# One-transfer gate fetches, variance scaling on GpSimd and a kept turned context in a four-layer transformer kernel

## The chip, the cores and the metric

The kernel runs on one core of a Trainium2 chip. The metric is the device time of one execution in microseconds (us); lower is better. The core has TensorE (PE; PEld is its weight load), VectorE (DVE), ScalarE (ACT), GpSimd (POOL) and SyncE (SP), which in this kernel issues every transfer, and 16 DMA engines that carry the transfers out.

## The reference: what is computed

All data is float32. `x` is 128 batches x 64 tokens x 128 features, `ctx` (the context) has the same shape, `cond` is one vector of 128 features for each batch. Four blocks follow each other, each with weights of its own:

```
L0:  x += P(attn(ada(x), ada(ctx)))                                   ada = layer norm, scaled and shifted by silu(cond) @ W
L1:  x += g*P(self_attn(ada(x)));  x += P(attn(ln(x), ln(ctx)));  x += g*gelu_mlp(ada(x))
L2:  x += g*P(self_attn(ada(x)));  x += g*P(top16_attn(ada(x), ctx));  x += g*swiglu_mlp(ada(x))
L3:  x += g*P(self_attn(ada(x)));  x += P(attn(ln(x), ctx));  x += g*gelu_mlp(ada(x))
```

Every attention has 16 heads of 8 features over 64 keys. The gates `g` depend on `cond`, so on the batch and the feature and not on the token. There are seven of them. L0 and L1 normalize the context, L2 and L3 take it raw.

## The kernel before

**Tiling.** A chunk is 8 batches, 512 tokens, so there are 16 chunks. Token-major tiles are [128, 4, 128]: partition = token of two neighbouring batches (64 tokens each), the middle index t = which pair of batches, then the feature. Feature-major ("turned") tiles are [128, 512]; `flip` (lines 612-621) makes one with four TensorE transposes. Most tiles come from a pool of 30 buffers of 256 KB named `some`; PSUM gives three slots named `mm`, two `ps` and one `po`.

**The order of the work** is not written out by hand. Each step is an `op(engine, cost, outs, ins, give, latency)`, given to a planner (`Plan`, lines 135-320) with a cost in ns and, for transfers, a latency. Eight lanes each work on one chunk and take the next when theirs runs out. `Plan.run` places, again and again, the step that can start first by those costs. It tries 48 seeds that vary the costs by 1% and keeps the shortest plan. Each engine then gets its instructions in the planned order, and keeps to it on the chip whatever the real durations are. Where the plan leaves TensorE idle for over 1000 ns, `warm` (line 1138) puts dummy matmuls into about half of the gap. Changing any cost, or taking any step out, so gives another order everywhere.

**A layer norm** is `moments` (line 633: two batch-norm statistics on DVE), then in `normal` one DVE instruction over 128x4 elements that makes variance + eps (line 645), a power of -1/2 on POOL (line 648, `minus_half` is a constant tile), four DVE instructions that normalize (line 653), and `flip`. `modulate` scales on DVE (line 662, out of PSUM) and shifts on POOL (line 663). There are 12 norms a chunk, two of them of the context.

**The context** is loaded from DRAM by `context` four times a chunk, once a layer (line 610). L0 and L1 take moments and normalize; L2 and L3 only flip it (tile `pc`) and copy it out of PSUM on ACT (line 1065).

**Attention** projects keys, queries and values, sends the queries through four transfers that spread them over a block tile (line 696, `qbd`), makes scores (line 741) and exponentials (line 752), or for the top-16 attention a chain of DVE maximum searches (lines 809-824), and weighs the values (line 871). Result and softmax sums leave PSUM on ACT (line 881), go to a DRAM tile `spill` (line 882) and come back by head (sums at line 899, values at line 903). DVE takes the reciprocal of the sums (line 906, tile `rec`), which goes to DRAM (line 908, `spillrec`) and comes back broadcast over the 8 features of a head (line 912: the DRAM side is walked as [16, 8 times the same, 512], the other side as 128 partitions). POOL multiplies (line 916). `watch` (lines 929-931) keeps on POOL, for a test at the end, a running sum of the reciprocals and a count of those above 2^-100. If the test fails, a slower safe version of the network runs as well; in the profiled run it did not.

**Gates.** `prepare` computes each of the seven gates once and stores it to DRAM as [128 batches, 2, 128]: part 0 is the gate, part 1 the gate times the projection's bias (line 550, one store a gate). `by_token` (lines 940-950) fetches one part for a chunk into a `some` tile, broadcast over the tokens. It issues two transfers on SP (line 947), one for the even and one for the odd batches, each walked as [64 times the same, 4, 128] on the DRAM side and 64 partitions on the other. `add` (line 962) uses part 1 on POOL, `residual` (lines 970-971) part 0 on DVE with a POOL addition behind it. That makes 14 fetches a chunk, 224 in all, as 448 transfers. The fetch of part 1 waits for the statistics of the norm ahead of it, that of part 0 for the reciprocal of the attention's sums or for the second half of the MLP.

Every transfer of the kernel goes through one queue that SP issues in the planned order, and SP waits at each transfer until what that transfer needs is there.

Of the kernel before, what the change touches and what calls it, by code (L numbers as in the profile page):

```python
# [21 lines left out]
NCHUNK = B // CB  # L22
NT = T // P
NPAIR = CB // 2
N_ATTN = 7
TOPK = 16
MLP = 512
LANES = 8
# [2 lines left out]
NSOME = 30  # L31
NQBD, NPROB, NVAL = 3, 8, 4
SCALE = 1.0 / math.sqrt(HD)
REC_HI, REC_LO = 2.0**64, 2.0**-100
GONE = -(2.0**126)


# [287 lines left out]
def kernel(ctx: ExitStack, tc: tile.TileContext, ins: dict, out: bass.AP, nchunk: int = NCHUNK):  # L325
# [13 lines left out]
        )  # L339


    ident = const.tile([P, P], F32, name="ident")
    make_identity(nc, ident)
    ones = const.tile([P, P], F32, name="ones")
    nc.gpsimd.memset(ones, 1.0)
    minus_half = const.tile([P, NT], F32, name="minus_half")
    nc.gpsimd.memset(minus_half, -0.5)


    cond_in = const.tile([P, D], F32, name="cond_in")  # L350
# [3 lines left out]
    bm1h = const.tile([P, NJ], F32, name="bm1h")  # L354
    scT = const.tile([P, B], F32, name="scT")
    dram = ctx.enter_context(tc.tile_pool(name="dram", bufs=1, space=bass.MemoryType.DRAM))
    gates_dram = [dram.tile([B, 2, D], F32, name=f"gates{n}") for n in range(len(GATES))]
    mods, W, plain, col, at = {}, {}, {}, {}, 0
    for name, n in BIASES:
        col[name] = at  # L360
# [21 lines left out]
    def prepare(plan, ready, all_of_it, vblocks, queries, pool, spills):  # L382
# [23 lines left out]
        def scratch(width):  # L406
            t = plan.tile(lambda: pool[t.slot][:, :width], "some")
            return t

        def mm(name):  # L410
            return plan.tile(lambda: mm_tile(name), "mm")
# [44 lines left out]
        for layer in range(4):  # L456
# [72 lines left out]
            for n, (key, i, w, b, bv) in enumerate(GATES):  # L529
                if key != of:  # L530
                    continue
                bname, kinds = next((bname, kinds.split()) for k, _, bname, kinds in CONDS if k == key)
                cw, g, p, done = weights[key, i - i % 4], scratch(2 * D), mm("pg"), plan.kept(True)

                def products(cw=cw, i=i, p=p, bname=bname, w=w, b=b, bv=bv):
                    nc.tensor.matmul(
                        p()[:, :D], lhsT=scT, rhs=cw()[:, i % 4 * P : (i % 4 + 1) * P], start=True, stop=False
                    )
                    spread_bias(p()[:, :D], bname, i, False)
                    added(p()[:, D : 2 * D], w, b, bv)  # L540

                def keep(g=g, p=p, half=kinds[i] == "half"):
                    nc.vector.tensor_copy(g()[:, :D], p()[:, :D])
                    nc.vector.tensor_tensor(g()[:, D:], g()[:, :D], p()[:, D : 2 * D], ALU.mult)
                    if half:
                        nc.vector.tensor_scalar_mul(g()[:, :D], g()[:, :D], 0.5)

                op(PE, 900, [p], [cw, sc, bi, biases, *([ready_w[w]] if w else [])], products, bulk=late)
                op(DVE, 600, [g], [p], keep, bulk=late)
                op(SP, 400, [done], [g], lambda n=n, g=g: nc.sync.dma_start(  # L550
                    out=gates_dram[n].rearrange("b k d -> b (k d)"), in_=g()
                ), 2500, bulk=late)
                parts.append(done)

            op(SP, 1, [ready[layer]], parts, lambda: None)
        return plan.ops
# [13 lines left out]
    def lane(n, plan, work, safe, acc, ready, vblocks, queries, pool, spills):  # L570
# [6 lines left out]
        def wop(engine, cost, outs, takes, *rest, **how):  # L577

            op(engine, cost, outs, [*takes, ready[layer[0]]], *rest, **how)

        def sb(shape, tag, bufs=1):
            name = f"{tag}{n}"
            return plan.tile(lambda: work.tile(shape, F32, tag=name, name=name, bufs=bufs), name, bufs)
# [31 lines left out]
        def flip(x, name):  # L615

            p = mm(name)

            def turn():
                for t in range(NT):  # L620
                    nc.tensor.transpose(p()[:, t * P : (t + 1) * P], x()[:, t, :], ident)  # L621

            op(PE, 460, [p], [x], turn)
            return p

        def moments(x):


            parts = sb([P, NT, 3], "parts")

            def stats():
                for t in range(0, NT, 2):
                    nc.vector.bn_stats(  # L633
                        parts()[:, t : t + 2, :].rearrange("p t k -> p (t k)"),
                        x()[:, t : t + 2, :].rearrange("p t d -> p d t"),
                    )

            op(DVE, 740, [parts], [x], stats)
            return parts

        def normal(x, mv, eps):

            rstd = sb([P, NT], "rstd", 2)

            op(DVE, 238, [rstd], [mv], lambda: nc.vector.tensor_scalar(  # L645
                rstd().unsqueeze(2), mv()[:, :, 2:3], 1.0 / D, eps, ALU.mult, ALU.add
            ))
            op(POOL, 1070, [rstd], [rstd], lambda: nc.gpsimd.tensor_tensor(rstd(), rstd(), minus_half, ALU.pow))  # L648
            xn = some([P, NT, D])

            def norm():
                for t in range(NT):
                    nc.vector.tensor_scalar(  # L653
                        xn()[:, t, :], x()[:, t, :], mv()[:, t, 1:2], rstd()[:, t : t + 1], ALU.subtract, ALU.mult
                    )

            op(DVE, 1480, [xn], [x, mv, rstd], norm)

            return flip(xn, "pn")
# [15 lines left out]
        def attention(hq, hkv, wq, bq, wk, wv, topk=False):  # L675
# [250 lines left out]
            if not safe:  # L926

                def watch():
                    nc.gpsimd.tensor_scalar(fits, recs(), REC_LO, None, ALU.is_ge)
                    nc.gpsimd.tensor_tensor(acc[0], acc[0], recs(), ALU.add)  # L930
                    nc.gpsimd.tensor_tensor(acc[1], acc[1], fits, ALU.add)

                op(POOL, 1080, sums[:2], [recs], watch)
                if topk:
                    op(POOL, 320, [sums[2]], [counts], lambda: nc.gpsimd.tensor_tensor(
                        acc[2], acc[2], counts(), ALU.add
                    ))
            return oT

        def by_token(n, part, c, behind):  # L940

            g = some([P, NT, D])

            def fetch():
                for e in range(2):
                    rows = gates_dram[n][c * CB + e : (c + 1) * CB : 2, part, :]
                    nc.sync.dma_start(
                        out=g()[e * S : (e + 1) * S], in_=rows.unsqueeze(0).to_broadcast([S, NT, D])
                    )

            wop(SP, 1300, [g], behind, fetch, 2500)
            return g

        def add(x, gate, c, parts):
# [89 lines left out]
        def chunk(c):  # L1044
# [10 lines left out]
            def scaled(key, scale, shift):  # L1055
                return mods[key, scale], mods[key, shift], c

            def context(behind, eps=None, *scaled):

                ct, ck = load(c_flat, c, behind=behind), some([P, T])  # L1060
                pn = flip(ct, "pc") if eps is None else normal(ct, moments(ct), eps)
                if scaled:
                    modulate(ck, pn, *scaled)
                else:
                    op(ACT, 585, [ck], [pn], lambda: nc.scalar.copy(ck(), pn()))
                return ck
# [63 lines left out]
    def network(lanes, safe, acc=None):  # L1130
        def warm(tile, ns):
# [4 lines left out]
            while columns > 0:  # L1136
# [2 lines left out]
                columns -= n  # L1139

        slots = {"mm": 3, "ps": 2, "po": 1, "qbd": 1 if safe else NQBD, "prob": 2 if safe else NPROB,
                 "values": 1 if safe else NVAL, "some": 10 if safe else NSOME, "spill": 1 if safe else LANES}

        def planned(seed, tc=None, work=None, *tiles):
            plan = Plan(tc, slots, warm, seed)
# [6 lines left out]
        with tc.tile_pool(name=f"work{int(safe)}", bufs=1) as work:  # L1152


            vblocks = []
            for k in range(slots["values"]):
                v = work.tile([P, NPAIR * NH * VW + 32 - VW], F32, tag=f"vbuf{k}", name=f"vbuf{k}", bufs=1)
                vblocks.append(v)

            queries = []  # L1160
            for k in range(slots["qbd"]):
                q = work.tile([P, 4, T], F32, tag=f"qbd{k}", name=f"qbd{k}", bufs=1)
                queries.append(q)
            pool = [work.tile([P, T], F32, tag=f"some{k}", name=f"some{k}", bufs=1) for k in range(slots["some"])]
            spills = [
                (
                    dram.tile([NG, P, 2, P], F32, name=f"spill{int(safe)}_{k}"),
                    dram.tile([NH, T], F32, name=f"spillrec{int(safe)}_{k}"),
                )
                for k in range(slots["spill"])  # L1170
            ]
            assert planned(seed, tc, work, vblocks, queries, pool, spills) < math.inf

    acc = [const.tile([P, m], F32, name=k) for k, m in (("recsum", 4 * NH), ("fitting", 4 * NH), ("taken", 8))]
    fits = const.tile([P, 4 * NH], F32, name="fits")
    for a in acc:
        nc.gpsimd.memset(a, 0.0)
    network(LANES, False, acc)
# [2 lines left out]

    ok = const.tile([P, 8 * NH + 8], F32, name="ok")
    nc.vector.tensor_scalar(ok[:, 0 : 4 * NH], acc[0], REC_HI, None, ALU.is_le)
    nc.vector.tensor_scalar(ok[:, 4 * NH : 8 * NH], acc[1], float(N_ATTN * nchunk), None, ALU.is_equal)
    nc.vector.tensor_scalar(ok[:, 8 * NH :], acc[2], float(8 * TOPK * nchunk), None, ALU.is_equal)
    ok1 = const.tile([P, 1], F32, name="ok1")
    nc.vector.tensor_reduce(ok1, ok, AX.X, ALU.min)
# [33 lines left out]
```

## Time and profile before

| what | value |
|---|---|
| median of 3 runs (lowest to highest) | 1953.83 us (1948.8 to 1966.26) |
| the profiled execution's own time | 1960.57 us |
| its span | 1958.8 us |
| granted TensorE clock, mean | 0.956 |
| ACT busy, share of the span | 1265.2 us, 65% |
| POOL busy | 1139.4 us, 58% |
| ctx loads | 64 of 256 KB |
| gate transfers | 448 of 128 KB, median 3.5 us from issue to landing |

How to read it: a line of a group gives the busy time of all its instructions, the mean of one, and the idle time of the engine just before them with what ended it. A matmul counts twice there when it runs in two passes. A line of a wait gives who waited for whom, the total in us, how often and the longest. "SPq" is the issuing of a transfer by SP; the time to landing is counted from there until its data has arrived. A table by stage gives for each stretch of the span the busy time of each engine, the granted clock, the mean busy share of the 16 DMA engines and the GB/s they moved.

### The profile page before, as it was taken

To read this page: it belongs to the slowest core of one execution; us is meant where nothing else is said; L and a number is where in the kernel's file an instruction comes from. 1 tells how busy PE (TensorE), PEld (TensorE's weight loads), DVE (VectorE), ACT (ScalarE), POOL (GpSimd) and SP (SyncE) were. 2 spreads that over 40 slices of the span, in tenths; PEclk is the share of its full clock that TensorE was granted. 3 is DMA by queue.
4 is the path that set the end of the run, shared out by engine and by line. 5 is a ranking of instruction groups with operands and counts; after the bars stand their busy time and mean duration, and the time that the engine had idled before them with its cause. 6 is when DMAs were issued, how large, how long until landed. Compare 5 with 4: busy or idle time off the path is not lost. (4 is left out here: it accounts for less than half of the span.)

```text
span 1958.8 us, 75790 instructions
## 1 busy us (share of the span) xinstructions
PE 1732.5 (88%) x30631; PEld 1198.4 (61%) x30631; DVE 1446.4 (74%) x6299; ACT 1265.2 (65%) x1842; POOL 1139.4 (58%) x1226
## 2 busy tenths in 40 slices
PE   6798899889898898889989898889988899988987
PEld 4566666666566665666666666556656666656554
DVE  7635354899999899998634578867869989997411
ACT  1567677676577465766668577666775777665542
POOL 6535375656646755667646566657557556656432
PEclk7999899999999899999999998999999999999999
DMA  7345555443236332555455554445453435334332
GB/s 207 101 141 152 154 150 154 132 116 110 83 89 182 97 99 73 158 147 146 139 156 142 156 149 130 126 135 140 118 166 94 114 105 143 116 91 121 105 92 61
DMA packets 385339, 249.40 MB, mean 127 GB/s; under 512 B 56076, under 2 KB 341076, under 8 KB 384980
## 3 DMA queue, kind: packets, MB, share of 16 engines
q1 hardware_dynamic: 384980, 244.46, 43.6%
q8 instruction: 244, 4.00, 0.9%
q14 instruction: 115, 0.94, 0.2%
HBM read 147.49 MB, written 67.50 MB: 110 GB/s over the span
## 5 line engine op out<-in xcount | busy, mean ns | idle before, releaser
L752 ACT ACTIVATE prob<-ps 128x1024 f32<-128x1024 f32 x384 | 377.5, 1023 | 110.6 <-PE ps L741 109.3
L653 DVE TENSOR_SCALAR some<-x,parts,rstd 128x128 f32<-128x128 f32 x640 | 260.2, 469 | 56.9 <-POOL rstd L648 53.3
L871 PEld LDWEIGHTS po<-prob,vbuf 128*32 128x32 f32 x14336 | 219.3, 112 | 97.1 <-issue 51.4
L871 PE MATMUL po<-prob,vbuf 128*32 128x64 f32 x14336 | 259.4, 225 | 6.3 <-ACT prob L752 3.5
L648 POOL TENSOR_TENSOR rstd<-rstd,minus_half 128x4 f32<-128x4 f32 x192 | 200.2, 1047 | 91.4 <-DVE rstd L645 78.2
L916 POOL TENSOR_TENSOR some<-some,some 128x512 f32<-128x512 f32 x112 | 144.3, 1290 | 177.7 <-DMA some<-spillrec 107.2
L741 PE MATMUL ps<-qbd,some 32*64 32x256 f32 x6144 | 229.6, 394 | 10.5 <-DMA qbd<-some 4.4
L839 POOL TENSOR_TENSOR some<-some,some 128x512 f32<-128x512 f32 x128 | 166.8, 1306 | 114.4 <-ACT some L831 113.0
L971 POOL TENSOR_TENSOR x<-x,some 128x512 f32<-128x512 f32 x112 | 146.0, 1304 | 108.6 <-DVE some L970 96.8
L811 DVE MATCH_REPLACE8 some<-m,some 128x64 f32<-128x64 f32 x1024 | 206.4, 209 | 0.3 <-issue 0.3
L962 POOL TENSOR_TENSOR x<-x,some 128x512 f32<-128x512 f32 x112 | 147.1, 1315 | 84.3 <-DMA some<-gates 30.3
L714 ACT COPY vbuf<-pv 64x512 f32<-64x512 f32 x224 | 153.8, 687 | 51.7 <-PE pv L707 49.4
L881 ACT COPY some<-po 128x512 f32<-128x512 f32 x224 | 131.8, 589 | 82.6 <-PE po L871 59.5
L813 DVE MAX8 m<-some 128x8 f32<-128x64 f32 x1024 | 177.0, 214 | 0.0
L809 DVE MAX8 m<-some 128x8 f32<-128x64 f32 x1024 | 172.1, 209 | 4.3 <-ACT some L789 4.3
L970 DVE TENSOR_TENSOR some<-py,some 128x512 f32<-128x512 f32 x112 | 76.5, 683 | 119.4 <-PE py L983 34.2
L741 PEld LDWEIGHTS ps<-qbd,some 32*64 32x64 f32 x6144 | 119.1, 133 | 74.2 <-issue 28.4
L906 DVE RECIPROCAL rec<-sums 128x64 f32<-128x64 f32 x112 | 61.0, 545 | 132.6 <-DMA sums<-spill 132.5
L663 POOL TENSOR_TENSOR some<-some,mod_L 128x512 f32<-128x512 f32 x112 | 118.2, 1057 | 55.2 <-DVE some L662 46.6
L621 PE MATMUL pn<-ident,some 128*128 128x128 f32 x768 | 128.2, 285 | 20.6 <-DVE some L662 5.6
L621 PEld LDWEIGHTS pn<-ident,some 128*128 128x128 f32 x768 | 91.3, 142 | 82.4 <-issue 24.4
L633 DVE BATCH_NORM_STATS2 parts<-x 128x6 f32<-128x256 f32 x320 | 120.2, 417 | 16.1 <-POOL x L971 14.3
(209 smaller groups left out, 3585.2 us busy)
## 6 DMA issues: line engine op xcount, KB each, us to landing
spill<-some SPq DMA_DIRECT2D x224, 256.0 KB, 3.6
some<-gates SPq DMA_DIRECT2D x448, 128.0 KB, 3.5
qbd<-some SPq DMA_DIRECT2D x448, 64.0 KB, 2.1
some<-spill SPq DMA_DIRECT2D x112, 256.0 KB, 3.6
some<-spillrec SPq DMA_DIRECT2D x112, 256.0 KB, 4.0
some<-in_ctx_dram SPq DMA_DIRECT2D x64, 256.0 KB, 4.5
x<-in_x_dram SPq DMA_DIRECT2D x16, 256.0 KB, 2.9
out_dram<-x SPq DMA_DIRECT2D x16, 256.0 KB, 2.4
```

Source lines behind the costliest of these rows:

```text
L621: nc.tensor.transpose(p()[:, t * P : (t + 1) * P], x()[:, t, :], ident)
L648: op(POOL, 1070, [rstd], [rstd], lambda: nc.gpsimd.tensor_tensor(rstd(), rstd(), minus_half, ALU.pow))
L653: nc.vector.tensor_scalar(xn()[:, t, :], x()[:, t, :], mv()[:, t, 1:2], rstd()[:, t : t + 1], ALU.subtract, ALU.mult)
L714: nc.scalar.copy(v4(vbuf())[rows, :, :, 0 : 2 * HD].rearrange("p m h (d b) -> p m h d b", b=2)[:, :, :, :, b], pv()[rows].rearrange("p (m ...
L741: nc.tensor.matmul(pscs[g // 2]()[b * S : (b + 1) * S, g % 2, u].rearrange("p (h q) -> p h q", h=4), lhsT=kT()[rows, cols], rhs=qbd()[rows ...
L752: op(ACT, 1020, [pr], [psc], lambda pr=pr, psc=psc: nc.scalar.activation(pr().rearrange("p g u h q -> p (g u h q)"), psc().rearrange("p g ...
L809: nc.vector.max(m1()[:, j, :], ex()[:, j, :])
L811: nc.vector.match_replace(w()[:, j, :], m1()[:, j, :], ex()[:, j, :], GONE)
L813: nc.vector.max(m2()[:, j, :], w()[:, j, :])
L839: op(POOL, 1310, [ex], [ex, w], lambda ex=ex, w=w: nc.gpsimd.tensor_tensor(ex(), ex(), w(), ALU.mult))
L871: nc.tensor.matmul(po()[32 * j : 32 * j + 32, g, u], lhsT=vbuf()[:, at : at + 32], rhs=prs[gp]()[:, gi, u, j], start=True, stop=True,)
L962: op(POOL, 1310, [x], [x, g], lambda: nc.gpsimd.tensor_tensor(x(), x(), g(), ALU.add), bulk=True)
```

## The change

Gates: the DRAM tile becomes [16 chunks, 2 parities, 2 parts, 4, 128], with the gate of the even and of the odd batches of a chunk lying apart, so each half of a token tile reads one run of 512 floats (2048 B). It is written by four stores a gate (28 instead of 7), and a fetch is one transfer: the DRAM side is walked as [2, 64 times the same, 512], the other side as 128 partitions. The planner's numbers for it go from 1300 + 2500 ns to 690 + 2800 ns.

Variance + eps moves from DVE to POOL, into one step with the power (1250 ns instead of 238 and 1070). `minus_half` is filled earlier.

Context: L0's moments of the context are kept for L1. L2 stores its turned context to DRAM (a tile `turned` for each lane), and L3 loads that instead of loading, flipping and copying again.

`watch` keeps a sum of the reciprocals and a sum of the softmax sums (two additions instead of a comparison and two additions); the test at the end becomes that both stay under a bound.

```diff
-    gates_dram = [dram.tile([B, 2, D], F32, name=f"gates{n}") for n in range(len(GATES))]
+    gates_dram = [dram.tile([NCHUNK, 2, 2, NT, D], F32, name=f"gates{n}") for n in range(len(GATES))]
...
-                op(SP, 400, [done], [g], lambda n=n, g=g: nc.sync.dma_start(
-                    out=gates_dram[n].rearrange("b k d -> b (k d)"), in_=g()
-                ), 2500, bulk=late)
-                parts.append(done)
+                for e in range(2):
+                    for k in range(2):
+                        part = plan.kept(True)
+                        op(SP, 500, [part], [g], lambda n=n, g=g, e=e, k=k: nc.sync.dma_start(
+                            out=gates_dram[n][:, e, k], in_=g()[e::2, k * D : (k + 1) * D]
+                        ), 2500, bulk=late)
+                        parts.append(part)
...
-            op(DVE, 238, [rstd], [mv], lambda: nc.vector.tensor_scalar(
-                rstd().unsqueeze(2), mv()[:, :, 2:3], 1.0 / D, eps, ALU.mult, ALU.add
-            ))
-            op(POOL, 1070, [rstd], [rstd], lambda: nc.gpsimd.tensor_tensor(rstd(), rstd(), minus_half, ALU.pow))
+            def root():
+                nc.gpsimd.tensor_scalar(rstd().unsqueeze(2), mv()[:, :, 2:3], 1.0 / D, eps, ALU.mult, ALU.add)
+                nc.gpsimd.tensor_tensor(rstd(), rstd(), minus_half, ALU.pow)
+
+            op(POOL, 1250, [rstd], [mv], root)
...
                 def watch():
-                    nc.gpsimd.tensor_scalar(fits, recs(), REC_LO, None, ALU.is_ge)
                     nc.gpsimd.tensor_tensor(acc[0], acc[0], recs(), ALU.add)
-                    nc.gpsimd.tensor_tensor(acc[1], acc[1], fits, ALU.add)
-
-                op(POOL, 1080, sums[:2], [recs], watch)
+                    nc.gpsimd.tensor_tensor(acc[1], acc[1], cs(), ALU.add)
+
+                op(POOL, 690, sums[:2], [recs, cs], watch)
...
             def fetch():
-                for e in range(2):
-                    rows = gates_dram[n][c * CB + e : (c + 1) * CB : 2, part, :]
-                    nc.sync.dma_start(
-                        out=g()[e * S : (e + 1) * S], in_=rows.unsqueeze(0).to_broadcast([S, NT, D])
-                    )
-
-            wop(SP, 1300, [g], behind, fetch, 2500)
+                rows = gates_dram[n][c, :, part].rearrange("e t d -> e (t d)")
+                nc.sync.dma_start(
+                    out=g().rearrange("p t d -> p (t d)"), in_=rows.unsqueeze(1).to_broadcast([2, S, NT * D])
+                )
+
+            wop(SP, 690, [g], behind, fetch, 2800)
...
+            seen, turned = [], plan.tile(lambda: spills[turned.slot][2], "turned")
+
             def context(behind, eps=None, *scaled):
 
+                if eps is None and turned.writer is not None:
+                    ck = some([P, T])
+                    op(SP, 500, [ck], [turned, *behind], lambda: nc.sync.dma_start(out=ck(), in_=turned()), 2600)
+                    return ck
                 ct, ck = load(c_flat, c, behind=behind), some([P, T])
-                pn = flip(ct, "pc") if eps is None else normal(ct, moments(ct), eps)
+                if eps is None:
+                    pn = flip(ct, "pc")
+                    op(ACT, 585, [ck], [pn], lambda: nc.scalar.copy(ck(), pn()))
+                    op(SP, 500, [turned], [ck], lambda: nc.sync.dma_start(out=turned(), in_=ck()), 2500)
+                    return ck
+                if not seen:
+                    seen.append(moments(ct, "seen"))
+                pn = normal(ct, seen[0], eps)
```

## The prediction

> **What bounds the kernel now.** I read the page's busy shares first, then the stages, then the waits, then the DMA lines.
>
> ```profile
> PE 1732.5 (88%) x30631; PEld 1198.4 (61%) x30631; DVE 1446.4 (74%) x6299; ACT 1265.2 (65%) x1842; POOL 1139.4 (58%) x1226
> ```
>
> TensorE is the busiest. 103.7 us of its time are the dummy matmuls of L1138. By stage (us; busy PE, PEld, DVE, ACT, POOL; clock, DMA share, GB/s):
>
> ```profile
> 100.00:400.00 300.00, 267.32 (x5432) 186.30 (x5431) 156.57 (x460) 211.84 (x292) 163.64 (x188) 0.96 0.52 148
> 400.00:900.00 500.00, 444.20 (x7954) 306.05 (x7955) 470.99 (x2474) 328.05 (x506) 308.66 (x316) 0.96 0.41 117
> 900.00:1200.00 300.00, 282.57 (x5289) 199.25 (x5288) 183.62 (x539) 215.34 (x299) 181.14 (x199) 0.97 0.51 146
> 1200.00:1500.00 300.00, 261.33 (x4886) 185.21 (x4878) 240.19 (x1098) 203.09 (x298) 183.69 (x201) 0.94 0.47 132
> 1500.00:1800.00 300.00, 269.72 (x4717) 188.32 (x4716) 274.74 (x1433) 205.97 (x313) 180.81 (x185) 0.97 0.41 116
> 1800.00:1959.00 159.00, 135.85 (x1520) 85.10 (x1518) 46.92 (x108) 64.61 (x89) 56.87 (x61) 0.95 0.29 84
> ```
>
> The reader is to see two co-limits, PE (about 90%) everywhere and DVE beside it in the top-16 stages (94% and 92%), and a DMA share near one half. That share is a mean over 16 engines: one engine can be full while it stays low.
>
> ```profile
> DVE rec L906 <- DMA sums<-spill: 132.5, 44, 12.3
> ...
> POOL some L916 <- DMA some<-spillrec: 107.2, 44, 7.1
> ...
> PEld py L983 <- POOL some L916: 92.4, 54, 6.0
> ```
>
> The attention's round trip through DRAM is already what DVE and POOL wait for most, and PE waits behind POOL: transfers have little slack.
>
> ```profile
> DMA packets 385339, 249.40 MB, mean 127 GB/s; under 512 B 56076, under 2 KB 341076, under 8 KB 384980
> ...
> q1 hardware_dynamic: 384980, 244.46, 43.6%
> ...
> some<-gates SPq DMA_DIRECT2D x448, 128.0 KB, 3.5
> ...
> some<-spillrec SPq DMA_DIRECT2D x112, 256.0 KB, 4.0
> ```
>
> And of the groups (line, shapes, times; busy us, mean ns; idle before):
>
> ```profile
> L645 DVE TENSOR_SCALAR rstd<-parts 128x4 f32<-128x4 f32 x192 | 63.1, 331 | 5.5
> ...
> L929 POOL TENSOR_SCALAR fits<-rec 128x64 f32<-128x64 f32 x112 | 45.6, 407 | 106.8 <-DVE rec L906 72.8 <-DVE m L809 21.3 <-DVE some L653 4.4
> ...
> L935 POOL TENSOR_TENSOR taken<-taken,counts 128x8 f32<-128x8 f32 x16 | 3.3, 204 | 9.3 <-DVE some L824 9.3
> ```
>
> From the packet counts one learns how many DMA engines a transfer uses. Of 56,076 packets under 512 B, 224 x 128 = 28,672 are the 256-byte pieces of the sums and of rec. That leaves 27,404 tiny closing packets. The program issues 1,713 transfers (1,671 of the groups named in the DMA view plus 42 loads of weights, cond and biases). At 16 each they would close with 27,408. Exactly four are missing. One transfer alone has a number of rows that 16 doesn't divide, the bias table with 72; the largest divisor of 72 up to 16 is 12. So a transfer is cut over a number of engines that divides its outermost count, and every other transfer of before has 16, 32, 64 or 128 there.
>
> **The change part by part.** Durations are of the profiled execution: span 1958.8, own time 1960.57, which is 0.3% above the median of 1953.83.
>
> *Gate fetch.* 448 transfers x 614 ns of issue (median of L947) leave SP and 224 come. Their issue costs about 546 ns (L912, the same size and also a broadcast), so SP issues 275 - 122 = 153 us less. SP waits for others anyway (267.9 us at L882 for ACT alone), so I book nothing on the path. The new source is walked as [2, 64, 512] and the target as 128 rows. If the outermost count decides as it did for the 72 rows, 2 is all that divides both sides, and one fetch of 262,144 B goes over two engines instead of 16. No transfer of before has 2 there, so the cost is bounded from both sides:
> - On 16 engines: the nearest row is spillrec, [16, 8, 512] onto 128 partitions, landing in 4.0 us. Against 3.5 that is +0.5 us a fetch, hidden: the two halves were issued one after the other, and one issue is now gone.
> - On two engines: 64 packets of 2,048 B on each. The trace's packet records give 84 ns (median) for such a packet, so 5.4 us. By the queue's mean, 0.436 x 16 x 1958.8 / 244.46 MB = 55.9 us per MB on one engine, 131,072 B take 7.3 us.
>
> I take two engines at 5.4 us: the packet count of this very trace shows the cut, and 2,048 B is the very packet size. Landing is then 3.5 + about 5 = 8.4 us. I assume that it is always the same two engines, which no row shows; with pairs that change no engine would fill, and the middle would be nearer to rival D.
>
> [...]
>
> Load of the two engines over the run: 224 x 5.376 = 1,204 us for gates (7.3: 1,635). The rest of the queue: 0.436 x 16 x 1958.8 = 13,665 us, minus the old gates (114,688 packets of 512 B at 28.9 ns = 3,313), minus 16 ctx loads (237), plus 32 turned transfers (344), over 16: 654 us. Sum 1,858 us, 95% of the span. By stage, with fetches counted by their users (L962 + L970: 35, 60, 36, 37, 39, then 17 at the end) and the rest from the DMA share minus 0.925 us a fetch for the old gates: 188 + 124 = 312 of 300; 323 + 150 = 472 of 500; 194 + 120 = 313 of 300; 199 + 107 = 306 of 300; 210 + 87 = 297 of 300. From 100 to 1800 us that is 1,700 us of work for 1,700 us. The other 14 engines fall to about 33%.
>
> No engine here keeps pace at 100%. All transfers share one queue, so qbd, spill, sums, rec and spillrec that are issued after a fetch stand behind it on these two engines, and SP, which waits in order, issues the next late. On POOL, an L962 that waits for its fetch holds the powers (L648), L916 and L663; on DVE, an L970 holds L653 and L906; PE waits for both. As the sustainable share I take what today's bound reaches: PE without dummies, (1,525 - 57) / 1,700 = 86% from 100 to 1800. The middle becomes 1,700 / 0.86 = 1,977 us (+277). In the last stage, 17 fetches land 4.9 us later each, between 0 and 83 us; of the 224 a user was seen waiting about 34 times, so about four count, +20. Ends: 95% share and nothing at the end, 1,789 in the middle (+89); 7.3 us a fetch, 1,700 + 207 x 1.92 = 2,098, at 86% 2,440 (+740); at 80% with 5.4 us, 2,125 (+425).
>
> *Gate stores*: 21 more x 0.33 us of issue (L550) = 7 us on SP in the first 110 us, between 0 and 7; SP's waiting there for DVE covers it; taken as 0.
>
> *Variance on POOL*: DVE loses 63.1 us. POOL gains 192 instructions between 204 ns (L935, 128x8, the nearest in size) and 407 (L929): 39 to 78 us. *Watch* takes 45.6 us (L929) away. POOL's net is -7 to +32 us on 1,139, no new bound. The power now stands behind POOL's queue already at the variance, which is 331 ns sooner done on DVE; in rank this is nothing beside 5 us.
>
> *Context kept*: 32 statistics x 0.417 = 13.4 us off DVE, 64 transposes = 10.0 us off PE, 16 ACT copies = 9.4 us off ACT. In the changed order ACT loads six tables more (67 against 61 in the work), 6 x 1.283 = 7.7 us back. 16 turned stores and 16 loads replace 16 ctx loads: counted above. Dummy columns fall from 49,222 to 46,944.
>
> What these small parts are worth where PE and DVE bound: 10.0 us on PE, and on DVE in the two top-16 stages 13.9 + 8.9 us (L645 there) and about 4 of the 13.4: up to 37 us, at least 0. With two DMA engines as the bound they are slack, and I book 0.
>
> Sum: 1,960.6 + 277 + 20 = 2,258 on the profiled execution; on the median's footing 2,250, and I say **2,240 us**, since part of the savings may count in the first and last stage.
>
> **The rivals.**
> - B, the other side: the fetch spreads over 16 engines as all wide transfers of before did. Then SP, DMA (3,313 us of packets become 2,408), DVE and PE all have less to do, and up to 37 us come off: 1,960 - 35 = 1,925. For it: spillrec is a broadcast and lands in 4.0 us. Against it: its outer count is 16. It decides if engines in use are more than about four: at four, a fetch takes 2.7 us on each and their load is 654 + 602 = 1,256 us, 64%, which fits.
> - C, the same but the savings lie beside PE's dummies and the planner's new order costs what it saves: within 1%, about 1,950. For it: PE stays near 90% and gives up 10 us.
> - D, two engines, but prefetch hides most: fetches are asked for well ahead of their use. Middle at 95% share: 1,960 + 89 = 2,050. Against it: the two engines delay every other transfer too.
> - E, the two engines move a byte as slowly as the queue's mean: up to 2,700.
>
> **How the numbers follow.** A with 2,240 has 0.70 (its own range 2,080 to 2,560), D 0.08, E 0.06, B 0.10, C 0.06. A measurement of this kernel tells about 1% from no change. Faster by over 1% is B, 0.10; within 1% is C, 0.06; slower by over 1% is A, D and E, 0.84. For 8 in 10 the range takes A nearly whole, D and the part of C above 1,950, and leaves out B and the top of E: 1,950 to 2,560.
>
> **What would show it.** Right: some<-gates x224 landing at 8 us or more; sums, spill and spillrec landing later than 2.4, 3.6 and 4.0; the waits of L906 and L916 for transfers grown several times; mean DMA share about 35 to 40% all the same; PE near 77%; closing packets 14 short of 16 for each of the 224 fetches. Small parts: L645 gone, a POOL instruction of about 0.2 us in its place. Wrong: gates landing near 4 us, or PE still near 90% with a longer span, which would put the blame on the new order.

## The result and the profile after

| what | before | after |
|---|---|---|
| median | 1955.5 us (1948.8 to 1966.26, 4 runs) | 2468.66 us (2465.04 to 2475.0, 4 runs) |
| ratio | 1 | 1.2621, 95% interval 1.2557 to 1.2685 |
| span of the profiled execution | 1958.8 us | 2466.1 us |
| granted TensorE clock, mean | 0.956 | 0.872 |

The kernel is 26% slower. The lines of the page of the kernel after that answer to those shown of before, busy times first:

```profile
PE 1865.3 (76%) x30559; PEld 1272.3 (52%) x30559; DVE 1366.0 (55%) x6075; ACT 1267.8 (51%) x1832; POOL 1128.6 (46%) x1306
...
DMA packets 289991, 253.53 MB, mean 103 GB/s; under 512 B 49948, under 2 KB 212964, under 8 KB 289636
...
q1 hardware_dynamic: 289636, 248.63, 33.1%
```

No engine is the bound any more: PE fell from 88% to 76% of the span and DVE from 74% to 55%. The mean share of the DMA engines fell as well, from 43.6% to 33.1%, so a reader who looks only at that mean will look elsewhere. The packet count tells where. Of 49,948 packets under 512 B, 28,672 are pieces of sums and rec as before, and 21,276 are closing packets (4 B each in the trace's records). The changed program issues 1,526 transfers. With 16 closing packets for 1,301 of them, 12 for the bias table and 2 for each of the 224 fetches, that makes 20,816 + 12 + 448 = 21,276, to the packet.

The waits of the kernel after (who waited for whom: total us, times, longest):

```profile
POOL x L963 <- DMA some<-gates: 316.7, 69, 12.2
DVE rec L909 <- DMA sums<-spill: 286.9, 68, 21.7
POOL some L919 <- DMA some<-spillrec: 247.0, 51, 15.5
PEld py L984 <- POOL some L919: 195.5, 57, 12.2
DVE some L971 <- DMA some<-gates: 192.5, 34, 13.2
```

The same waits for the gates in the kernel before:

```profile
DVE some L970 <- DMA some<-gates: 32.1, 11, 6.4
POOL x L962 <- DMA some<-gates: 30.3, 15, 3.7
```

POOL's wait for the gates rose from 30.3 to 316.7 us and DVE's from 32.1 to 192.5. But transfers that were not touched come late too: sums from 132.5 to 286.9, spillrec from 107.2 to 247.0. The page gives no time to landing for this kernel, so the waits stand for it. Two stretches of the timeline of after, SP's issuing and POOL (start, duration, what; in brackets the idle time before and what ended it):

```profile
1299.18 0.56 SPq L948 DMA_DIRECT2D some<-gates  x1
...
1300.30 0.55 SPq L948 DMA_DIRECT2D some<-gates  x1
1300.97 3.36 SPq L915 DMA_DIRECT2D some<-spillrec  x1
1304.37 0.49 SPq L948 DMA_DIRECT2D some<-gates  x1
1305.20 5.21 SPq L885 DMA_DIRECT2D spill<-some  x1
```

```profile
1313.80 1.26 POOL L919 TENSOR_TENSOR some<-some,some 128x512 f32<-128x512 f32 x1 [10.28 <-DMA some<-spillrec]
1318.93 1.27 POOL L963 TENSOR_TENSOR x<-x,some 128x512 f32<-128x512 f32 x1 [3.87 <-DMA some<-gates]
```

Two gate fetches go out at 1299.18 and 1300.30, two times 5.4 us of work for their engines by the prediction's packet time (64 packets at 84 ns, an estimate). The spillrec load behind them, usually 0.56 us of issue, holds SP for 3.36 us. After the next fetch a spill store, usually 0.4, holds SP for 5.21 us. POOL sits idle for 10.28 us, until 1313.80, before the spillrec load issued at 1300.97 is there, and later 3.87 more for a gate. That is the damage in one picture: the fetch is in front, and what the others need stands behind it.

The trace's packet records show the same from the side of the engines. From 1307.5 to 1318 us some 25 packets of 2,048 B start in each us, two in flight at a time, which is what two engines make at 84 ns a packet. The fetches issued at 1300.30 and 1304.37 are both outstanding; on different pairs, four of their packets would be in flight. They go one after the other, with closing packets up to 1312.53 and 1318.34. The spill store issued at 1305.20 goes past them on the other engines: 448 of its 512 packets of 512 B start between 1310.5 and 1312 us, and 14 closing packets follow by 1311.95. Its last 64 packets start only from 1318.11 on, when the second of these fetches is ending, and its last closing packet stands at 1319.10. The sums load, which waits for that store, goes out at 1319.51. Over the whole run exactly two packets of the queue are in flight for 847.3 us, against 54.6 us in the kernel before.

### The profile page after: what moved, and what is told of

It reads as the page before. It is cut to its first block, busy times and chain, and to the rows that moved or that the text cites. A ratio compares the mean times of both kernels' runs of the same rounds, so it can differ in the third digit from the quotient of the medians.

```text
span 2466.1 us, 75200 instructions
## 1 busy us (share of the span) xinstructions
PE 1865.3 (76%) x30559; PEld 1272.3 (52%) x30559; DVE 1366.0 (55%) x6075; ACT 1267.8 (51%) x1832; POOL 1128.6 (46%) x1306
## 2 busy tenths in 40 slices
DMA packets 289991, 253.53 MB, mean 103 GB/s; under 512 B 49948, under 2 KB 212964, under 8 KB 289636
## 3 DMA queue, kind: packets, MB, share of 16 engines
q1 hardware_dynamic: 289636, 248.63, 33.1%
## 5 line engine op out<-in xcount | busy, mean ns | idle before, releaser
L963 POOL TENSOR_TENSOR x<-x,some 128x512 f32<-128x512 f32 x112 | 144.5, 1290 | 347.8 <-DMA some<-gates 316.7
L919 POOL TENSOR_TENSOR some<-some,some 128x512 f32<-128x512 f32 x112 | 143.5, 1282 | 347.1 <-DMA some<-spillrec 247.0
L874 PEld LDWEIGHTS po<-prob,vbuf 128*32 128x32 f32 x14336 | 234.9, 118 | 104.1 <-issue 67.0
L874 PE MATMUL po<-prob,vbuf 128*32 128x64 f32 x14336 | 275.6, 233 | 5.7 <-ACT prob L755 2.9
L971 DVE TENSOR_TENSOR some<-py,some 128x512 f32<-128x512 f32 x112 | 76.3, 687 | 362.5 <-DMA some<-gates 192.5
L744 PE MATMUL ps<-qbd,some 32*64 32x256 f32 x6144 | 238.9, 411 | 5.5 <-ACT prob L755 3.1
L909 DVE RECIPROCAL rec<-sums 128x64 f32<-128x64 f32 x112 | 61.3, 548 | 287.3 <-DMA sums<-spill 286.9
L623 PE MATMUL pn<-ident,some 128*128 128x128 f32 x768 | 140.1, 303 | 49.5 <-DVE some L656 21.7
L623 PEld LDWEIGHTS pn<-ident,some 128*128 128x128 f32 x768 | 99.8, 152 | 121.3 <-issue 41.7
L688 ACT COPY some<-pk 128x512 f32<-128x512 f32 x112 | 65.6, 588 | 171.5 <-PE pk L686 144.7
```

Of the source, the lines that this page charges most:

```text
L744: nc.tensor.matmul(pscs[g // 2]()[b * S : (b + 1) * S, g % 2, u].rearrange("p (h q) -> p h q", h=4), lhsT=kT()[rows, cols], rhs=qbd()[rows ...
L874: nc.tensor.matmul(po()[32 * j : 32 * j + 32, g, u], lhsT=vbuf()[:, at : at + 32], rhs=prs[gp]()[:, gi, u, j], start=True, stop=True,)
```

## The experiments

Theory 1: the fetch runs on two DMA engines, and all that stands behind it on them is held. Theory 2: the new order, or the three small parts, cost the time. Theory 3: only the gates themselves come late. Each run was compared with the kernel before on the same chip.

### The same kernel, the fetch on 16 engines again (e1_halves)

```diff
-                nc.sync.dma_start(out=g()..., in_=rows.unsqueeze(1).to_broadcast([2, S, NT * D]))
+                for e in range(2):
+                    nc.sync.dma_start(out=g()[e * S : (e + 1) * S]..., in_=rows[e].unsqueeze(0).to_broadcast([S, NT * D]))
```

> The changed kernel with its fetch cut into two transfers again, each walked as [64 times the same, 512] onto 64 partitions; layout, planner numbers and the order of the instructions stay. Theory 1 (the fetch runs on two DMA engines and fills them): the slowdown goes, 1,900 to 1,960 us. Theory 2 (the new order or the three small parts cost it): it stays above 2,300. Theory 3 (only the gates themselves come late, other transfers are not held): also 1,900 to 1,960, so this run does not tell 1 from 3.

Measured: 1968.5 us, ratio 1.0067 (1.0034 to 1.0099). By the packet records its 27,996 closing packets are 16 for each of its 1,750 transfers, less the four of the bias table. All engines have the order of the changed kernel, instruction for instruction, and still the whole loss is gone but 0.7%. Theory 2 falls for the 26%. The time is a little above the 1,960 I gave as the upper end: the small parts show no gain here.

### The gate part alone (e2_gates_only)

```diff
+                rows = gates_dram[n][c, :, part].rearrange("e t d -> e (t d)")
+                nc.sync.dma_start(out=g()..., in_=rows.unsqueeze(1).to_broadcast([2, S, NT * D]))   # the rest as before
```

> The kernel before with the gate part of the change alone (layout, four stores, one transfer). Theories 1 and 3: 2,400 to 2,550 us, about as slow as the whole change. Theory 2: 1,930 to 2,000.

Measured: 2512.17 us, ratio 1.2859 (1.282 to 1.2898). The gate part is enough to make all of the loss; the order here is another one again.

### Four and sixteen engines (e3_k4, e4_k16)

```diff
-    gates_dram = [dram.tile([NCHUNK, 2, 2, NT, D], ...
+    gates_dram = [dram.tile([NCHUNK, 2, 2, R, NT, D], ...          # R = 2 or 8 copies of each row
-                    in_=rows.unsqueeze(1).to_broadcast([2, S, NT * D])
+                    in_=rows.unsqueeze(1).to_broadcast([2 * R, S // R, NT * D])     # rows: (parity, copy)
```

> The changed kernel, gates stored twice, so that the one transfer is walked as [4, 32 times the same, 512]: the same bytes, by theory 1 over four engines. Load of these by the sum of the prediction: 654 + 602 = 1,256 us, some 64% of the span. Theory 1: 1,940 to 2,030 us, most of the slowdown gone at once, since four engines no longer fill. Theory 3: the extra landing time halves and with it the loss, 2,100 to 2,250. Theory 2: 2,468.

> The changed kernel, gates stored eight times, so that the one transfer is walked as [16, 8 times the same, 512]: by theory 1 over 16 engines. Theories 1 and 3: as e1_halves or up to 10 us less, since SP issues 224 transfers fewer, 1,895 to 1,955 us. Theory 2: 2,468. The stores grow from 28 to 112, some 30 us of SP's issuing spread over the first part.

Measured: e3_k4 2096.74 us, 1.0724 (1.0687 to 1.0761); e4_k16 1992.74 us, 1.0195 (1.0118 to 1.0271). The line of e3_k4's page that gives its engines:

```profile
DMA packets 292680, 254.46 MB, mean 121 GB/s; under 512 B 50844, under 2 KB 215652, under 8 KB 292324
```

50,844 - 28,672 = 22,172 closing packets, which is 1,329 x 16 + 12 + 224 x 4: four engines. Both runs missed their numbers. With four engines I expected at most 2,030. Their load by the prediction's sum is 1,256 us, 60% of the 2,094.6 of the span, and they still cost 6.5% over e1_halves: an engine need not be full to hold others up. The doubled gate stores are a small part of that: all engines have the order of e1_halves, and at the matmul that e1_halves starts at 176 us e3_k4 is 22 us behind it, at the last one 135. For e4_k16 I had put its stores at 30 us without loss. By stage its loss lies at the start, where the 112 stores stand on SP; e1_halves first, then e4_k16:

```profile
100.00:200.00 100.00, 87.69 (x1967) 61.39 (x1968) 36.48 (x95) 68.64 (x95) 50.32 (x66) 0.95 0.54 151
```

```profile
100.00:200.00 100.00, 55.48 (x1049) 39.84 (x1048) 23.95 (x55) 38.03 (x52) 28.61 (x38) 0.76 0.50 137
```

PE does 55 us of work there instead of 88. From 113.6 to 171.9 us SP issues 80 of the 112 stores, 54.8 us of issuing with little in between. At the matmul that e1_halves starts at 176 us, e4_k16 is 56 us behind; its span is 37.9 us longer in all. So the stores cost more than the whole loss in these two executions, and 18 us came back behind them. Whether the halved issue on SP gave these 18 us stays open, as the executions of each of the two kernels spread by 26 and 29 us.

### Loaded engines without late gates (e5_load, e9_load16)

```diff
+                # e1_halves, and behind the two halves, into DRAM tiles that nobody reads:
+                nc.sync.dma_start(out=beside[k], in_=rows.unsqueeze(1).to_broadcast([2, S, NT * D]))               # e5_load
+                nc.sync.dma_start(out=beside[k]..., in_=sixteen_rows.unsqueeze(1).to_broadcast([16, 8, NT * D]))   # e9_load16
```

> e1_halves, its gates on 16 engines, and beside each fetch one more transfer of 256 KB from DRAM to DRAM, walked as [2, 64 times the same, 512], that nobody waits for (work added; nothing left out). It loads two DMA engines as the changed kernel does, while the gates themselves take the short way. Theory 1 (the two full engines hold every transfer that stands behind): 2,350 to 2,650 us, with the waits for sums, spillrec and gates all grown. Theory 3 (it was only the gates' own late landing): 1,970 to 2,030.

> Control for e5_load: the same added 256 KB from DRAM to DRAM beside each fetch, but walked as [16, 8 times the same, 512] (work added; nothing left out). Same bytes, same issues, same order, 16 engines. Theory 1: the bytes are harmless when spread, 1,970 to 2,040 us. If the added traffic or the added issues as such were the cause in e5_load: above 2,300.

Measured: e5_load 2586.8 us, 1.33 (1.3248 to 1.3352); e9_load16 2088.68 us, 1.0688 (1.0652 to 1.0724). The waits of e5_load, then of e9_load16:

```profile
DVE rec L910 <- DMA sums<-spill: 407.2, 81, 21.8
POOL some L920 <- DMA some<-spillrec: 368.0, 64, 17.0
PEld py L989 <- POOL some L920: 332.1, 69, 12.5
```

```profile
DVE rec L910 <- DMA sums<-spill: 181.6, 56, 22.9
POOL some L920 <- DMA some<-spillrec: 180.9, 54, 11.3
PEld py L993 <- POOL some L920: 127.0, 54, 6.7
```

This pair decides between theories 1 and 3. In both kernels the gates themselves go over 16 engines and nobody needs the added data; the same bytes are added by the same number of issues. The 28,444 closing packets of e5_load are 448 more than those of e1_halves, two for each added transfer; the 31,580 of e9_load16 are 3,584 more, 16 for each. On two engines instead of 16 they cost a ratio of 1.33 - 1.0688 = 0.261 more. In the changed kernel against e1_halves, where the gates are late as well, it is 1.2621 - 1.0067 = 0.255. Theory 3 allowed at most 2,030 us for e5_load and falls: a load on two engines that nobody waits for makes a loss of the same size. The gates do come later in e5_load too, since they stand behind the added transfers like all else: DVE and POOL wait 92.1 and 82.0 us for them, against 29.4 and 53.7 in e9_load16 (192.5 and 316.7 in the kernel after). How much of the loss of the kernel after comes by the gates and how much by the other held transfers was not separated. The spread bytes were not harmless, though: 2,089 against the 2,040 that I gave as the upper end, 6.2 points above e1_halves. What of that is the 224 added issues and what the traffic was not separated.

### An order that knows of the late gates (e10_told)

```diff
-            wop(SP, 690, [g], behind, fetch, 2800)
+            wop(SP, 690, [g], behind, fetch, 8000)
```

> The changed kernel with the planner told 8,000 ns instead of 2,800 for the landing of a fetch, so that it makes an order in which gates may come late. Theory 1a (two full engines and what stands behind them): little helps, since sums, spill and spillrec still land late, 2,380 to 2,500 us. Theory 1b (a third or more of the loss comes from an order that trusts 2,800 ns): 2,100 to 2,300.

Measured: 2429.46 us, 1.2417 (1.237 to 1.2463). About 39 of 513 us come back, as theory 1a said. Its waits fit that theory:

```profile
POOL some L919 <- DMA some<-spillrec: 434.6, 71, 14.8
DVE rec L909 <- DMA sums<-spill: 314.0, 66, 23.1
```

The gates are gone from the head of the list, and the held transfers have taken their place.

### What the small parts are worth (e6_dve_var, e7_other_seeds, e8_context_only, e11_halves_told, e12_same_order)

```diff
-            op(POOL, 1250, [rstd], [mv], root)                              # e6: e1_halves, variance back on DVE
+            op(DVE, 238, [rstd], [mv], variance); op(POOL, 1070, [rstd], [rstd], power)
-        seed = 0 if safe else min(range(TRIES), key=planned)                # e7: the kernel before, nothing else
+        seed = 0 if safe else min(range(TRIES, 2 * TRIES), key=planned)
+            seen, turned = ...                                              # e8: the kernel before with the context part
-            wop(SP, 690, [g], behind, fetch, 2800)                          # e11: e1_halves
+            wop(SP, 1300, [g], behind, fetch, 2500)
-            op(DVE, 238, [rstd], [mv], variance)                            # e12: the planner sees the old steps,
+            op(DVE, 238, [rstd], [mv], lambda: None)                        #   POOL's step does variance and power;
-                op(POOL, 1080, sums[:2], [recs], watch)                     #   old cost, watch in two additions;
+                op(POOL, 1080, sums[:2], [recs, cs], watch)                 #   new gate layout, fetched in two halves
```

> e1_halves with the variance back on DVE in front of the power on POOL; the planner makes another order. Theory P (the variance in POOL's queue eats what the other small parts give): 1,925 to 1,950. Theory Q (the small parts lie off the path and the order decides within 1%): 1,945 to 1,975, as e1_halves.

> The kernel before with the planner trying seeds 48 to 95 instead of 0 to 47: the same work in another order. It measures how far an order alone moves the time. Theory Q: up to 1% either way, 1,935 to 1,975. If it stays within 0.2%, a difference of 0.7% as in e1_halves is not the order's.

> The kernel before with the context part alone (moments kept, turned tile stored and loaded). By the prediction's rows 10.0 us less on PE and 13.4 on DVE: up to 20 us faster, 1,935, if they lie on the path; by theory Q 1,940 to 1,970.

> e1_halves with the planner told the old numbers 1300 and 2500 for its two transfers; another order again, the same work. Theory Q: 1,940 to 1,985, anywhere in the spread of orders. Were the wrong numbers what costs e1_halves its gain: 1,915 to 1,935.

> The kernel before in exactly its own order of instructions (the planner still believes the old costs), with the new gate layout fetched in two halves, the variance on POOL and the watch in two additions. DVE loses 63 us, POOL 46 and gains about 39, the gates' packets become a quarter in number. Theory Q (these savings are real and the new order hides them): 1,925 to 1,942 us, faster than before by 0.3 to 1.2%. Theory R (they lie off the path): 1,943 to 1,955, the same.

| run | median us | ratio | 95% interval |
|---|---|---|---|
| e6_dve_var | 1990.17 | 1.0226 | 1.0192 to 1.026 |
| e7_other_seeds | 1973.35 | 1.0135 | 1.009 to 1.0181 |
| e8_context_only | 1969.95 | 1.0127 | 1.0092 to 1.0162 |
| e11_halves_told | 1956.85 | 1.0022 | 0.9992 to 1.0052 |
| e12_same_order | 1946.11 | 0.9965 | 0.9946 to 0.9984 |

e7_other_seeds is the ruler. It does exactly the work of the kernel before, and another order alone makes it 1.35% slower. Against that, e6, e8 and e11, which all have orders of their own, say little of their edits. e6 missed both its ranges, and e8 stands at the very end of theory Q's: with less work they are slower than before. Only e12_same_order holds the order fixed. There variance, watch and gate layout together give 0.35%, some 7 us, and it is the one version that beats both kernels. Its time lies in theory R's range and its ratio at the lower end of theory Q's: the saving is clear of the noise and small beside the busy time that was taken away. Its busy times, and the DVE row that the variance left behind:

```profile
PE 1733.5 (89%) x30631; PEld 1199.8 (62%) x30631; DVE 1403.8 (72%) x6107; ACT 1266.3 (65%) x1842; POOL 1130.4 (58%) x1306
```

```profile
L658 DVE TENSOR_SCALAR some<-x,parts,rstd 128x128 f32<-128x128 f32 x640 | 272.7, 487 | 84.0 <-POOL rstd L650 80.5 <-ACT some L886 1.4 <-PE pv L712 1.0
```

DVE has 42.6 us less to do, not 63. The normalizing instruction behind the power now takes 487 ns instead of 469, which is 12.5 us of the difference; the rest was not followed. It also waits 80.5 us for the power instead of 53.3. The context part was never run in the old order, so its own worth stays open.

## Why the prediction was right, and where its sizes were off

- *Two engines a fetch*: right. The closing packets show 2 for each fetch in the kernel after, and 4 in e3_k4.
- *Always the same two*: right. From 1307.5 to 1318 us two fetches follow each other on one pair, and the spill store, 448 of whose 512 packets have passed, waits for the same pair with its last 64 until 1318.11; with exactly two packets in flight for 847.3 us of the run, this is no single case. Which two of the 16 they are, the records don't tell.
- *What stands behind is held, on every engine in the chain named*: right, in the waits (sums 132.5 to 286.9 us, spillrec 107.2 to 247.0), and shown by e5_load and e9_load16 for a load that is not the gates' (sums 407.2 us on two engines, 181.6 on 16).
- *The sustainable share*: this is the term that was mis-sized. I took 86%, today's share of PE, and got 277 us for the middle; the loss is 513 us in all. Instruction by instruction against e1_halves, which has the same order, the kernel after falls 480 us behind between 100 and 1800 us of e1_halves and 23 us in the rest, where I had 277 and 20. (The 20 was close partly by luck: 34 waits in 224 give two or three late fetches of 17, not four.) The two engines' own work came out as summed: the rest of the queue, 0.331 x 16 x 2466.1 = 13,060 us minus 2,408 for the gates, over 16, is 666 us, and with 1,204 for the gates 1,870 against 1,858 forecast (both at 84 ns a packet). But that is 76% of the span, and for 464 us of the run no packet of the queue was in flight at all. So the two engines were not kept full. My reading, which no run tests by itself: what they hold up comes so late that the next transfers are not asked for in time, and one fetch stops more than one of the eight lanes.
- *Rival B decides if engines are more than about four*: wrong in its number. Four engines have room by load (60%) and still cost 6.5%. The loss per fetch over e1_halves goes 2.2 us with two engines ((2,468 - 1,968) / 224) and 0.57 with four, its added stores included, where the fetch occupies its engines for an estimated 5.4 and 2.7 us (64 and 32 packets at 84 ns).
- *Rival B's 1,925 and the small parts' "up to 37 us"*: with 16 engines the time was 1,957 to 1,993 in the orders tried, and 7 us were found in the old order. The busy times moved as summed (DVE -80, POOL -11 in the changed kernel, the variance on POOL 195 ns by the median against 204 assumed), but most of them did not show in the time. That a new order can cost more than they give was in rival C only.
- *Gate stores as 0*: not contradicted for the 28 of the change (from 100 to 200 us PE is busy for 87.7 us in e1_halves, for 89.3 in the kernel before); for 112 it was wrong.
- *What would show it*: the DMA share came as 33% instead of 35 to 40. PE near 77% came as 76%, but by luck: the span was longer than forecast, and PE's own work grew with it. With its 1,732.5 us of before it would have been at 70%.

The step that nothing foresaw is the clock, below.

## What to carry to other kernels

Before merging two transfers into one, look at the outermost count of both sides: here a fetch walked as [2, 64, 512] onto 128 partitions closed with 2 packets (the kernel after), as [4, 32, 512] with 4 (e3_k4), the bias table of 72 rows with 12, and transfers with 16, 32, 64 or 128 there with 16. The mean DMA share, 33.1% in the kernel after, hid two engines that held up a whole queue. Counting the closing packets against the number of transfers shows it. And where a planner orders the work, measure how far another order alone moves the time before believing a gain, or a loss, of a per cent: here it was 1.35%.

## What the runs showed of the hardware that was not expected

The granted clock followed how busy PE was, over these runs: 0.954 to 0.964 at 87 to 89% busy (the kernel before 0.956), 0.941 at 86% (e4_k16), 0.93 at 84% (e3_k4), 0.872 at 76% (after), 0.863 at 75% (e2_gates_only), 0.855 at 73% (e5_load). The traces' records of this clock hold two levels only, full and half (1.0 and 0.5). Half was granted for 174.6 us in the kernel before, in 34 stretches, for 171.2 us in e1_halves and for 632.3 us in the kernel after, in 90. With the same 30,559 matmuls in the same order as e1_halves, PE was busy 151.7 us longer (132.8 us longer than before, with 72 matmuls fewer). The planner's dummies fill planned gaps alone, and these gaps were not planned. In the 3.41 us ahead of each half-clock stretch, added up, PE was busy for 59.55 of 307.28 us in the kernel after, 19%, and for 38.35 of 116.03 in the kernel before, 33%, against 76% and 88% of the span. Inside the half-clock stretches of the kernel after a matmul of 128x512 (L1006) took 1,061 ns by the median of the trace's records, outside them 592. How much of the 513 us is this slower clock and how much waiting was not separated. The fetch is all that differs from e1_halves, so both come with it; that the waiting is what lowers the clock is my reading of these shares, and no run tests it by itself.

SP's issue of a transfer is not of fixed length. A spill store took at most 1.79 us to issue in the kernel before and up to 5.21 us behind the two-engine fetches (1.73 in e1_halves, which has the same order), so a held queue also delays whatever SP has next: the fetch behind the spillrec load of 3.36 us went out at 1304.37, when these had ended.
